# Softmax transpositions as two 64-row halves, and reciprocals broadcast by TensorE instead of by DMA

## The chip, the cores and the metric

The kernel runs on one NeuronCore of one Trainium2 chip. The metric is device time in microseconds for one execution. Besides, one execution was profiled: its span runs from its first to its last instruction.

## The reference

A stack of four graph layers over x of shape (32, 512, 64), in float32, all with one adjacency matrix `adj` (512 x 512). Each layer adds to x a function of h = max(layernorm(x), 0):

- layer 0: `h @ weight_self + adj @ h @ weight_neighbor + bias`
- layer 1: twice `z = relu(adj @ z @ W)`
- layer 2: graph attention. With `Wh = h @ W.T`, the scores are `leaky_relu(e1[i] + e2[j], 0.2)`, masked where adj is not positive; then a softmax over j, the product with Wh, and elu
- layer 3: eight attention heads. Each takes `g = h @ Wh[head]`, scores `(g @ g.T) * adj` with zeros masked, a softmax, and the product with g plus a bias; the heads are joined, go through leaky_relu, and one more layer of the same kind (8 x 128 to 64 features) gives the output, with leaky_relu on top.

So there is one softmax over 512 x 512 scores for each batch entry in layer 2, eight for each in layer 3's heads, and one for each in layer 3's output: 320 in all.

## The kernel before

Layers 0 and 1 run first (the loop from L215), over four groups of eight batch entries. All the rest is a pipeline of 160 *units*: 16 of `Gat` (layer 2, two batch entries each), 128 of `Heads` (two heads of one batch entry) and 16 of `Out` (two batch entries). A unit holds two softmaxes, numbered k = 0 and 1, and takes four steps, one for each block r of 128 score rows.

`run` (L609) writes out the steps of all units, each stage shifted: at a step, one unit makes its scores (`scores`, L469) and, at the end of the step, its row work (`soft`); an earlier one is transposed (`transpose`, L335); a yet earlier one is multiplied with its values (`values`, L348); and an older one is finished (`end`). `prep` readies the unit that comes next. This gives priorities; the framework under the kernel (Tile) then fixes each engine's order, gives out the buffers and sets the semaphores, so that the order in the trace isn't always that of the code.

The work of a flow step (Heads and Out):

- TensorE makes the scores of 128 rows, 2 x 512 columns, into `s_ps`: two matmuls with a contraction of 64, one on each row half of the array (L472). A plain float32 matmul shows as two records in the trace, a transposition as one.
- VectorE multiplies them with adj (`s_att`, L461), makes the mask (L465), and adds both with a row minimum for each k (L325, `finish_rows`).
- ScalarE takes the exponential, with the row sums on the way (L329), into `p_att`.
- For each column block j of 128, `transpose` makes eight 128 x 128 transpositions, four (r) for each k, into a PSUM bank `pt_ps` for each k (L341); ScalarE copies each bank to `pt_att` (L346).
- `values` adds up `av` over j: k = 0 in the first 64 output partitions, k = 1 in the others, so on the two column halves of the array (L353).
- `recips` (L358) is called with the first transposition block (j = 0): the reciprocals of the row sums (`rec`, 128 partitions x 2 x 4, L360) are stored to DRAM (L363) and loaded again, each k as one row of 512, repeated over 64 partitions (`recb`, L366, two loads). Both kinds of DMA are issued on the queue of SyncE (SP), where the stores of the result (L600) stand too.
- `normalize` (L373) multiplies `av` with `recb` to `o_att`. Then Heads makes `y_ps` from it (L544), which ScalarE turns into `cat` (L549).

PSUM has eight banks: two buffers of two banks for `s_ps`, one bank for `av`, and three for everything with the tag "m" (`ps_m`, L266): `pt_ps`, `y_ps`, `g_ps`, `gT_ps` and others.

Of the kernel before, what the change touches and what calls it, by code (L numbers as in the profile page):

```python
# [8 lines left out]
F32 = mybir.dt.float32  # L9
# [5 lines left out]
P = 128  # L15
# [7 lines left out]
def gnn_stack_kernel(  # L23
# [22 lines left out]
    nc = tc.nc  # L46
    B, N, F = x.shape
    C = N // P
# [59 lines left out]
    ident = const.tile([P, P], F32, name="ident")  # L108
# [12 lines left out]
    with tc.tile_pool(name="ps_setup", bufs=2, space=PSUM) as ps:  # L121
        for k in range(C):
            pt = ps.tile([P, N], F32, name="pt")
# [133 lines left out]
    def row_tile(name):  # L257
# [1 line left out]
        return wk.tile([P, N], F32, name=name, tag="row", bufs=2 * H + 6)  # L259

    wk = ctx.enter_context(tc.tile_pool(name="work_b", bufs=2))
    dram = ctx.enter_context(
        tc.tile_pool(name="dram", bufs=3, space=bass.MemoryType.DRAM)
    )
    ps_s = ctx.enter_context(tc.tile_pool(name="ps_s", bufs=2, space=PSUM))
    ps_m = ctx.enter_context(tc.tile_pool(name="ps_m", bufs=3, space=PSUM))  # L266
    ps_v = ctx.enter_context(tc.tile_pool(name="ps_v", bufs=1, space=PSUM))
# [12 lines left out]
    pt = ps_m.tile([P, H, F], F32, name="whT_ps", tag="m")  # L280
# [5 lines left out]
    for h in range(H):  # L286
        nc.tensor.matmul(
            pm[:, h],
            lhsT=whT[:, h].rearrange("p k f -> p (k f)"),
            rhs=whT[:, h, 0],  # L290
            start=True,
            stop=True,
# [12 lines left out]
    def halves(k):  # L305
        return slice(k * F, (k + 1) * F)

    class Pair:
# [26 lines left out]
        def transpose(self, j):  # L335
            pt = pbuf.tile([P, 2, N], F32, name="pt_att", bufs=3)
            self.pts = getattr(self, "pts", []) + [pt]
            for k in range(2):
                ps = ps_m.tile([P, N], F32, name="pt_ps", tag="m")
                for r in range(C):  # L340
                    nc.tensor.transpose(  # L341
                        ps[:, r * P : (r + 1) * P],
                        self.p[:, k, r, j * P : (j + 1) * P],
                        ident,
                    )
                nc.scalar.copy(pt[:, k, :], ps)  # L346

        def values(self, j):  # L348
            pt = self.pts.pop(0)
# [8 lines left out]
        def recips(self):  # L358
            rec = tiny.tile([P, 2, C], F32, name="rec")
            nc.vector.reciprocal(rec, self.sum)  # L360

            row = dram.tile([2, C, P], F32, name="rec_row")
            nc.sync.dma_start(row.rearrange("k r p -> p k r"), rec)  # L363
            self.recb = wk.tile([P, N], F32, name="recb")
            for k in range(2):
                nc.sync.dma_start(  # L366
                    self.recb[halves(k), :],
                    row[k : k + 1].rearrange("k r p -> k (r p)").to_broadcast([F, N]),
                )

        def normalize(self):
            self.o = wk.tile([P, N], F32, name="o_att")
# [236 lines left out]
    def run(units):  # L609
        units = units + [None] * 3  # L610

        def at(k, off):
            u, j = divmod(k - off, C)
            return (units[u], j) if 0 <= u < len(units) else (None, j)

        for j in range(C):
            units[0].prep(j)
        for k in range(len(units) * C):
            cur, r = at(k, 0)
            if cur:  # L620
                cur.scores(r)
            u, j = at(k, C + LAG)
            if u:
                u.transpose(j)
                if j == 0:
                    u.recips()
            u, j = at(k, C + LAG + 1)
            if u:
                u.values(j)
            u, j = at(k, 2 * C + LAG + 1)  # L630
            if u:
                u.end(j)
            u, j = at(k, -C)
            if u:
                u.prep(j)
            if cur:
                cur.soft(r)
# [4 lines left out]
    for b in range(B):  # L642
# [4 lines left out]
        if b % 2 == 1:  # L647
            due.append(((b + 1, 2), b - 1))
    order += [None, None, None, Out(B - 2)]
    run(order)  # L650


# [33 lines left out]
```

## Time and profile before

| What | Value |
|---|---|
| Median of 3 runs | 3047.99 us (3045.97 to 3050.04) |
| The profiled execution's own time | 3050.04 us |
| Its span | 3048.1 us |
| TensorE, busy share of the span | 90% (12972 matmul records) |
| VectorE | 80% (4802 instructions) |
| ScalarE | 63% (4426) |
| Mean granted TensorE clock | 0.955 |
| `pt_ps` transpositions (L341) | 5120, 738.4 us busy |
| `pt_att` copies (L346) | 1280, 578 ns each |
| `rec` (L360) | 160, 201 ns each |
| DMAs `rec_row` and `recb` | 160 and 320, 10.5 and 3.2 us from issue to landing |

The kernel has stages with different limits: layers 0 and 1 until about 460 us, Gat until about 705 us, heads and outputs until about 2985 us, and an end in which the last Out unit has nothing beside it. A line of the page's groups gives the code line, engine, operation, tiles written and read, shapes and count, then busy time and mean duration, then the idle time of the engine just before. In the timeline a row begins with its start and its length in microseconds. "PEld" is TensorE's loading of weights, which goes on beside its matmuls. TensorE's busy time is that of overlapping records whose ends are modelled: the time from one start to the next tells more.

### The profile page before, as it was taken

The numbers are of one execution on the slowest core, as the hardware profiler recorded it, in microseconds if no ns is written. First come the engines' busy times: TensorE is split into PE (matmuls) and PEld (weight loads), VectorE is DVE, ScalarE is ACT, GpSimd is POOL, SyncE is SP. The second block draws the span as 40 slices with busy tenths as digits, with TensorE's granted clock in tenths as the row PEclk, the third lists the DMA queues.
The fourth block names the chain that finished last, engine by engine and source line by source line (L and its number), as shares of the span: only waits on it lengthen the run. The fifth ranks groups of instructions, "written<-read, shape, count | busy, mean of one in ns | idle before, by whom it ended". The sixth has DMA issues, their size and how long they took to land.

```text
span 3048.1 us, 37087 instructions
## 1 busy us (share of the span) xinstructions
PE 2753.6 (90%) x12972; PEld 1251.4 (41%) x12972; DVE 2425.9 (80%) x4802; ACT 1933.2 (63%) x4426; POOL 99.5 (3%) x49
## 2 busy tenths in 40 slices
PE   4674667888899999999999999999999999999996
PEld 2332334444344444444444444444444444444442
DVE  5325337899898988889898989888898989898893
ACT  0110115667687777777777777777777777777773
POOL 3102100000000000000000000000000000000000
PEclk9887887899899999999999999999999999999998
DMA  3000000000110111111110101111011101011010
GB/s 82 0 0 0 0 0 8 15 15 15 15 22 15 25 18 18 22 18 22 18 22 18 22 18 22 20 20 18 19 22 18 22 18 22 18 22 22 18 22 14
DMA packets 201851, 55.42 MB, mean 18 GB/s; under 512 B 172488, under 2 KB 180848, under 8 KB 201536
## 3 DMA queue, kind: packets, MB, share of 16 engines
q1 hardware_dynamic: 198832, 49.97, 10.1%
q8 instruction: 101, 1.65, 0.3%
q10 hardware_dynamic: 2080, 2.10, 0.2%
q14 instruction: 86, 0.70, 0.2%
q0 software_dynamic: 752, 0.99, 0.2%
HBM read 48.17 MB, written 4.85 MB: 17 GB/s over the span
## 4 chain that ended last, share of the span: by engine, by line
DVE 55%; PE 24%; ACT 13%; issue 5%; DMA 2%; POOL 1%; POOLq 0%; DVEq 0%; SPq 0%; ACTq 0%
DVE t_att L325 18%; DVE s_att L461 14%; DVE t_att L465 8%; ACT p_att L329 8%; PE nt_ps L195 6%; PE av L353 3%; PE pt_ps L341 3%; DVE o_att L373 3%; ACT cat L549 3%; PE s_ps L472 3%; PE gT_ps L567 3%; PE po L206 2%; DVE l_att L432 2%; DVE hn L164 1%; DVE l_att L325 1%
## 5 line engine op out<-in xcount | busy, mean ns | idle before, releaser
L329 ACT ACTIVATE p_att<-t_att,negmax 128x512 f32<-128x512 f32 x1152 | 824.0, 716 | 459.7 <-DVE negmax L325 459.0
L461 DVE TENSOR_TENSOR s_att<-s_ps,adj_p 128x1024 f32<-128x1024 f32 x576 | 702.9, 1220 | 118.6 <-PE s_ps L472 118.6
L341 PEld LDWEIGHTS pt_ps<-ident,p_att 128*128 128x128 f32 x5120 | 554.2, 142 | 547.6 <-issue 230.5
L341 PE MATMUL pt_ps<-ident,p_att 128*128 128x128 f32 x5120 | 738.4, 283 | 28.1 <-ACT cat L549 10.5
L325 DVE CUSTOM_DVE_ANT_0 t_att<-s_att,t_att 128x512 f32<-128x512 f32 x1152 | 752.3, 687 | 13.3
L346 ACT COPY pt_att<-pt_ps 128x512 f32<-128x512 f32 x1280 | 678.6, 578 | 120.9 <-PE pt_ps L341 120.6
L472 PE MATMUL s_ps<-hx,g 64*128 64x512 f32 x2048 | 679.7, 627 | 1.4 <-DVE s_att L461 1.4
L353 PE MATMUL av<-pt_att,hn 128*64 128x512 f32 x2048 | 571.3, 618 | 0.7 <-DVE o_att L373 0.7
L465 DVE TENSOR_SCALAR t_att<-s_att 128x1024 f32<-128x1024 f32 x576 | 393.2, 683 | 24.5 <-ACT pt_att L346 0.9
L472 PEld LDWEIGHTS s_ps<-hx,g 64*128 64x128 f32 x2048 | 214.0, 186 | 310.6 <-issue 104.8
L329 ACT ACTIVATION_READ_ACCUMULATOR p_att<-t_att,negmax 128x1 f32 x1152 | 216.0, 188 | 0.0
L195 PE MATMUL nt_ps<-adj_t,hn 128*128 128x512 f32 x256 | 134.9, 668 | 60.5 <-DVE hn L168 60.5
L199 ACT COPY nt<-nt_ps 128x512 f32<-128x512 f32 x48 | 28.1, 585 | 237.6 <-PE nt_ps L195 237.6
L544 PE MATMUL y_ps<-o_att,wh_sb 64*128 64x512 f32 x512 | 163.1, 645 | 6.0 <-DVE o_att L373 4.1
L549 ACT ACTIVATE cat<-y_ps,bh 128x512 f32<-128x512 f32 x256 | 159.4, 671 | 8.8 <-PE y_ps L544 8.8
L353 PEld LDWEIGHTS av<-pt_att,hn 128*64 128x64 f32 x2048 | 105.8, 135 | 97.2 <-issue 89.7
L246 DVE SCALAR_TENSOR_TENSOR x<-po,x 128x256 f32<-128x256 f32 x32 | 12.1, 419 | 167.5 <-PE po L206 167.5
L516 PE MATMUL g_ps<-hx,m 64*128 64x512 f32 x256 | 143.7, 641 | 0.0
L373 DVE TENSOR_TENSOR o_att<-av,recb 128x512 f32<-128x512 f32 x160 | 109.5, 684 | 32.5 <-DMA recb<-rec_row 29.0
L152 ACT ACTIVATE std<-var,eps 128x32 f32<-128x32 f32 x16 | 5.1, 321 | 189.3 <-DVE var L150 189.3
L567 PE MATMUL gT_ps<-cat,wo_sb 128*64 128x512 f32 x512 | 122.6, 602 | 0.0
L360 DVE RECIPROCAL rec<-sum_att 128x8 f32<-128x8 f32 x160 | 32.1, 201 | 111.7 <-ACT p_att L329 111.7
(114 smaller groups left out, 2015.4 us busy)
## 6 DMA issues: line engine op xcount, KB each, us to landing
recb<-rec_row SPq DMA_DIRECT2D x320, 128.0 KB, 3.2
out_dram<-x SPq DMA_DIRECT2D x32, 128.0 KB, 10.1
rec_row<-rec SPq DMA_DIRECT2D x160, 4.0 KB, 10.5
x<-in_x_dram ACTq DMA_DIRECT2D x2, 1024.0 KB, 23.5
x<-in_x_dram SPq DMA_DIRECT2D x2, 1024.0 KB
adj_raw<-in_adj_dram SPq DMA_DIRECT2D x1, 1024.0 KB
wh_sb<-in_L_gnn_Wh_dram POOLq DMA_DIRECT2D x2, 256.0 KB, 7.8
wo_sb<-in_L_gnn_W_out_dram POOLq DMA_DIRECT2D x1, 256.0 KB, 8.3
```

What stands on the lines that cost most here:

```text
L195: nc.tensor.matmul(p, lhsT=lhs(k), rhs=adj_t[:, k, :], start=(k == 0), stop=(k == C - 1))
L325: nc.vector.tensor_tensor_reduce(out=ns[k], in0=s[k], in1=t[k], scale=-1.0, scalar=BIG, op0=OP.add, op1=OP.min, accum_out=self.negmax[:, k ...
L329: nc.scalar.activation(self.p[:, k, r, :], ns[k], AF.Exp, bias=self.negmax[:, k, r : r + 1], scale=-1.0, accum_out=self.sum[:, k, r : r + 1],)
L341: nc.tensor.transpose(ps[:, r * P : (r + 1) * P], self.p[:, k, r, j * P : (j + 1) * P], ident,)
L346: nc.scalar.copy(pt[:, k, :], ps)
L353: nc.tensor.matmul(self.av[halves(k), :], lhsT=self.v(k, j), rhs=pt[:, k, :], start=(j == 0), stop=(j == C - 1),)
L373: nc.vector.tensor_tensor(self.o, self.av, self.recb, OP.mult)
L461: nc.vector.tensor_tensor(s, ps, adj_f[:, r, None, :].to_broadcast([P, 2, N]), OP.mult)
L465: nc.vector.tensor_scalar(t, s, 0.0, FLOW_NEG, op0=OP.is_equal, op1=OP.mult)
L472: nc.tensor.matmul(u.s_ps[:, k], lhsT=g[halves(k), r * P : (r + 1) * P], rhs=x[halves(k), :], start=True, stop=True,)
L549: nc.scalar.activation(cat, ps, AF.Prelu, bias=bh[:, h : h + 1], scale=1.0, alpha=0.01)
L567: nc.tensor.matmul(self.gps[halves(k), :], lhsT=wo_sb[:, h, :], rhs=Heads.cat[b + k, h], start=(h == 0), stop=(h == H - 1),)
```

## The change

Two things change. First, each 128 x 128 transposition becomes two of 64 rows: rows 0 to 63 of `p_att` on the first row half of TensorE, rows 64 to 127 on the second, issued in turn. Each half has its own PSUM bank, which now holds both k, so two of ps_m's banks are written side by side; ScalarE still makes two copies of 512 columns, now one for each half, and each writes runs of 64 elements. Second, the reciprocals no longer go through DRAM. Eight matmuls a unit, with a column of `rec` repeated 64 times as the stationary operand and the identity as the moving one, put them on 64 partitions for each k, in a bank of ps_m, and ScalarE copies that bank to `recb`. `recips` is called with the second block (j = 1) instead of the first, after its transpositions. The DRAM pool goes.

```diff
         def transpose(self, j):
             pt = pbuf.tile([P, 2, N], F32, name="pt_att", bufs=3)
             self.pts = getattr(self, "pts", []) + [pt]
+
+            ps = [ps_m.tile([P, 2, C, F], F32, name="pt_ps", tag="m") for half in range(2)]
             for k in range(2):
-                ps = ps_m.tile([P, N], F32, name="pt_ps", tag="m")
                 for r in range(C):
-                    nc.tensor.transpose(
-                        ps[:, r * P : (r + 1) * P],
-                        self.p[:, k, r, j * P : (j + 1) * P],
-                        ident,
-                    )
-                nc.scalar.copy(pt[:, k, :], ps)
+                    for half in range(2):
+                        nc.tensor.transpose(
+                            ps[half][:, k, r],
+                            self.p[halves(half), k, r, j * P : (j + 1) * P],
+                            ident[halves(half), halves(half)],
+                        )
+            pth = pt.rearrange("p k (r half q) -> p k r half q", r=C, half=2)
+            for half in range(2):
+                nc.scalar.copy(pth[:, :, :, half, :], ps[half])
...
             nc.vector.reciprocal(rec, self.sum)
-
-            row = dram.tile([2, C, P], F32, name="rec_row")
-            nc.sync.dma_start(row.rearrange("k r p -> p k r"), rec)
+            ps = ps_m.tile([P, N], F32, name="rec_ps", tag="m")
+            for r in range(C):
+                for k in range(2):
+                    nc.tensor.matmul(
+                        ps[halves(k), r * P : (r + 1) * P],
+                        lhsT=rec[:, k, r : r + 1].to_broadcast([P, F]),
+                        rhs=ident,
+                        start=True,
+                        stop=True,
+                    )
             self.recb = wk.tile([P, N], F32, name="recb")
-            for k in range(2):
-                nc.sync.dma_start(
-                    self.recb[halves(k), :],
-                    row[k : k + 1].rearrange("k r p -> k (r p)").to_broadcast([F, N]),
-                )
+            nc.scalar.copy(self.recb, ps)
...
                 u.transpose(j)
-                if j == 0:
+                if j == 1:
                     u.recips()
```

More of the change, by code (lines that the diff above doesn't have):

```diff
@@ L261, in gnn_stack_kernel @@
     wk = ctx.enter_context(tc.tile_pool(name="work_b", bufs=2))
-    dram = ctx.enter_context(
-        tc.tile_pool(name="dram", bufs=3, space=bass.MemoryType.DRAM)
-    )
     ps_s = ctx.enter_context(tc.tile_pool(name="ps_s", bufs=2, space=PSUM))
@@ L360, in recips @@
             nc.vector.reciprocal(rec, self.sum)
-            row = dram.tile([2, C, P], F32, name="rec_row")
-            nc.sync.dma_start(row.rearrange("k r p -> p k r"), rec)
-            self.recb = wk.tile([P, N], F32, name="recb")
-            for k in range(2):
-                nc.sync.dma_start(
-                    self.recb[halves(k), :],
-                    row[k : k + 1].rearrange("k r p -> k (r p)").to_broadcast([F, N]),
-                )
+            ps = ps_m.tile([P, N], F32, name="rec_ps", tag="m")
[8 more added lines that the diff above has]
+                    )
+            self.recb = wk.tile([P, N], F32, name="recb")
+            nc.scalar.copy(self.recb, ps)
         def normalize(self):
```

## The prediction

> **What bounds the kernel now.** I read the page's slices first, to find the stages.
>
> ```profile
> PE   4674667888899999999999999999999999999996
> DVE  5325337899898988889898989888898989898893
> ACT  0110115667687777777777777777777777777773
> ```
>
> From slice 10 on nothing changes: that is the softmax over heads and outputs, about 705 to 2985 us. TensorE (PE) stands at 9 throughout, VectorE (DVE) at 8 to 9, ScalarE (ACT) at 7. So I asked for busy times in the middle of that stage, for all work and then for the transpositions alone; the columns are PE, PE's weight loads, DVE, ACT, POOL, then clock and DMA (the second row: PE, weight loads, ACT).
>
> ```profile
> 1000.00:2500.00 1500.00, 1485.12 (x7238) 641.96 (x7236) 1320.08 (x2616) 1132.91 (x2618) 0.00 (x0) 1.00 0.13 20
> 1000.00:2500.00 1500.00, 437.62 (x3096) 329.83 (x3096) 407.66 (x774) 1.00 0.13 20
> ```
>
> 3096 transpositions at eight a step are 387 steps, so a step lasts 1500/387 = 3.876 us. In it PE is busy 3.84, DVE 3.41, ACT 2.93. PE is the bound, with DVE 11% behind. The waits of the same window say what stops DVE:
>
> ```profile
> DVE rec L360 <- ACT p_att L329: 77.5, 87, 2.1
> DVE s_att L461 <- PE s_ps L472: 75.2, 97, 2.1
> PE pt_ps L341 <- ACT cat L549: 7.6, 24, 0.5
> ```
>
> Of DVE's 180 us of idle time, 77.5 (0.20 a step) is the reciprocal waiting for an exponential and 75.2 (0.19) is waiting for scores from PE; the other 27 (0.07) are gaps between dependent operations. PE hardly waits. DVE's own floor is therefore 3.41 + 0.07 = 3.48 us a step.
>
> Then the timeline, a step with nothing extra in it, to see how PE spends its time:
>
> ```profile
> 1537.29 0.20 DVE L360 RECIPROCAL rec<-sum_att 128x8 f32<-128x8 f32 x1 [0.69 <-ACT p_att L329]
> 1537.63 1.13 PE L472 MATMUL s_ps<-hx,g 64*128 64x512 f32 x4
> 1538.69 1.09 PE L341 MATMUL pt_ps<-ident,p_att 128*128 128x128 f32 x8
> 1539.72 1.08 PE L353 MATMUL av<-pt_att,gV 128*64 128x512 f32 x4
> 1540.72 1.13 PE L472 MATMUL s_ps<-hx,g 64*128 64x512 f32 x4
> 1540.72 0.30 PEld L472 LDWEIGHTS s_ps<-hx,g 64*128 64x128 f32 x4 [0.81 <-DVE s_att L461]
> ```
>
> Scores, transpositions and values take 1.06 + 1.03 + 1.00 = 3.09 us back to back, in three array shapes: 64 rows, 128 by 128, 64 columns. In the single records the two halves of a score start 6 to 8 ns apart, their weight loads too: 4 loads of 185 ns fill 0.30 us. A transposition follows the last by 0.109 us. The last score record to the first transposition is 0.520, where a 512-column record needs 0.43 (the spacing of the weight loads of L195): the change of shape costs 0.09. The first transposition then takes 0.166, and the last is followed by the values after 0.202, again 0.09 over.
>
> One place already has the form that the change uses, a 64-row transposition, on one row half:
>
> ```profile
> L282 PEld LDWEIGHTS whT_ps<-ident,wh_sb x8: 136/138/143, 451.1 to 451.5; 64*128 64x128 f32 x8
> L282 PE MATMUL whT_ps<-ident,wh_sb x8: 221/223/244, 451.1 to 451.6; 64*128 64x64 f32 x8
> ```
>
> Each is one matmul record, and their starts are 0.062 us apart.
>
> **What the Trainium skill says.** "TensorEngine Tiling (Array Packing)", section "Key Properties": changing the tiling mode drains TensorE, and different tiles load weights and multiply in parallel. The trace agrees with both: 0.09 us at each change of shape, and score halves that start 6 to 8 ns apart. Its section "Gotcha 1: PSUM Pressure" says that row tiles write to different banks; the scores do so already. "TensorE: Matmul & The Clock Gate", section "Step-by-step: what each phase is for", gives a 64-deep queue from which weight loads are pulled ahead; the 6 to 8 ns after long matmuls fit. Its section "Wait — 56ns, not 53.3ns?" gives about 62 ns per matmul when the sequencer decodes in software. That is the whT pitch too, and those eight came straight after a blocking wait; so no row here tells whether 62 ns is the array or the sequencer.
>
> **The change part by part**, per step.
>
> *Transpositions.* Out: 8 of 0.109 with their switch in. From the last score record to the first value record there are 0.520 + 0.166 + 6 x 0.109 + 0.202 = 1.54 us, less 0.43 for the score itself: 1.11. In: 16 halves in 8 pairs, in the score's own shape, so no drain before them: 7 x 0.062 + (0.062 + 0.09) = 0.59. Saved: 0.53. Unknown is whether two halves overlap in transpose mode. If fully, 0.59; if not at all, 15 x 0.062 + 0.15 = 1.08, and 0.03 is saved. I take the first, because the score halves overlap in loads and matmuls and the shape is the same; the 32 instructions are queued behind a 1.06 us score. The shape changes from transposed to plain matmuls at one array size cost nothing in the trace (0.111 from e_ps to pt_ps).
>
> *ACT's copies* stay two of 0.58, now to runs of 64 elements; no row shows that form, so 0 to 10% more (an estimate), and I take 0: ACT has 0.9 us of slack in a step. The first copy began after four transpositions (0.5 us) and now begins after all sixteen (0.5 us as well).
>
> *Banks.* A step's transpositions need two of ps_m's three banks at their start, where the second was needed half-way. In the step after y_ps this waits for cat already now (7.6 us in 387 steps). All 16 then wait, but they need only 0.5 after it where the four left needed 0.43: about nothing. If ACT is late elsewhere, up to 0.1 a step.
>
> *Reciprocals on PE.* Eight matmuls a unit, two records each by the pattern of the other plain matmuls, 128 columns at 0.109: 16 records, in pairs on the two column halves as L353's values run, 8 x 0.109 = 0.87 us a unit, 0.22 a step (0.44 if the pairs don't overlap). They stand before the values, in their shape: no further switch. ACT gains one copy of 0.58 a unit, 0.15 a step.
>
> *The wait that this adds.* The first of them waits for DVE's reciprocal; behind it in PE's queue stand values, g_ps and the next scores, and for those waits DVE's s_att. The timeline has the reciprocal between s_att and t_att of a step, early; and recips moves from j = 0 to j = 1, a step later. So PE should find it done. The same move may shrink the 0.20 wait of the reciprocal on ACT; I keep 0.14 of it.
>
> *DMAs.* One store and two loads a unit leave SP's queue; SP then holds only the stores of out. They were hidden but for three places:
>
> ```profile
> DVE o_att L373 <- DMA recb<-rec_row: 29.0, 3, 14.2
> 3041.41 0.69 DVE L373 TENSOR_TENSOR o_att<-av,recb 128x512 f32<-128x512 f32 x1 [14.24 <-DMA recb<-rec_row]
> ```
>
> At the last the values were done at 3035.15, so 6.3 us were the DMA's; at 2999.89 3.4 were. With PE's 0.9 in their place: 8 us saved in all.
>
> **The sum.** PE's floor becomes 3.84 - 0.53 + 0.22 = 3.53, DVE's stays 3.48, ACT's is 3.07. Two engines within 0.05 of each other, with steps that differ (y_ps and g_ps add about 1 us to two of four), don't both run full. I put the step at DVE's 3.48 + 0.14 (reciprocal) + 0.07 (a third of the wait for scores) = 3.69: 0.185 less. Between 705 and 2985 us there are 4680/8 = 585 steps: 108 us. The Gat stage (460 to 705 us) has DVE busy 211 of 245 us, and its PE work isn't the bound: 0, within 10. The span is 3048.1 - 108 - 8 = 2932. The profiled execution took 3050.0, 2 us more than its span and 2 more than the median of the runs, so the median to expect is 2932 too.
>
> **Rivals.** (1) *The halves don't overlap*, or the sequencer feeds one in 62 ns. PE: 3.84 - 0.03 + 0.22 + 0.04 = 4.07, 0.19 more, 585 times: +111 - 8, 3151 us. For it: no transposed pair is in the trace, and whT's 62 ns. Against it: the scores. It decides once a pair takes over 0.105 us; there the gain is gone. (2) *The reciprocal's wait takes the place of the DMA*: if DVE has it behind the whole row work of the step before, PE may only do that step's scores and transpositions (1.06 + 0.59) under it. A unit is then 4 x 3.53 - 1.65 + 3.1 (row work) + 0.2 + 0.3 for hand-overs = 16.1 us against 15.5: 0.14 a step, 3130 less 8, about 3120. It decides when PE waits over 1.4 us a unit. Against it: the reciprocal's place at 1537.29. (3) *DVE keeps all its waits or the three banks bind*: step 3.80 to 3.86, 2995 to 3042 us. (4) *Both engines run full*: 3.56, 2855 us; the lower end.
>
> **How the numbers follow.** Likeliest, halves overlap and DVE takes over, 0.67, with its own range of 2855 to 2995; (3) 0.08; no change 0.03 (within 0.2%, 6 us, about what a measurement of this kernel can tell from none); (1) 0.13; (2) 0.09. Faster 0.75, same 0.03, slower 0.22. The range 2860 to 3080 leaves out 0.03 below, (1), and a part of (2).
>
> **What would show it.** Right: 16 records of pt_ps in about 0.55 us with pairs 6 to 8 ns apart, 0.43 from the last score to the first of them, PE busy below 3.7 a step, and DVE with the highest share. Wrong: half records spaced 0.06 singly (1); PE idle at the new matmuls before a reciprocal (2); pt_ps waiting on pt_att, g or cat for over 0.1 a step (3). An order of instructions that differs much from today's would upset the sum in ways that I can't price.

## The result, and the profile after

The changed kernel takes 3201.45 us (median of 4 runs, 3199.80 to 3202.94), the kernel before in the same comparison 3048.57: **1.050 times as long** (95% interval 1.048 to 1.052). I had forecast 2932. The profiled execution took 3201.84 us, its span 3200.1.

The slices of the page show that no engine is full any more; from slice 10 on TensorE stood at 9 before.

```profile
PE   4666578778888889888889888888888898989887
DVE  5334438889878887878887888878788878888884
```

The middle of the long stage, all work and then the transpositions alone (columns as in the prediction):

```profile
1000.00:2500.00 1500.00, 1324.11 (x11086) 649.34 (x11082) 1234.20 (x2439) 1093.84 (x2530) 0.00 (x0) 1.00 0.01 3
1000.00:2500.00 1500.00, 324.05 (x5792) 268.97 (x5790) 381.91 (x722) 1.00 0.01 3
```

5792 halves at 16 a step are 362 steps of 4.144 us, where before there were 387 of 3.876. TensorE is busy 161 us less in the window, and the steps are 0.27 longer all the same. The waits of that window say what filled the time:

```profile
DVE rec L361 <- ACT p_att L326: 169.7, 80, 2.1
PE g_ps L520 <- ACT pt_att L347: 89.4, 80, 1.2
DVE s_att L465 <- PE s_ps L476: 68.9, 91, 2.6
PE pt_ps L340 <- ACT pt_att L347: 43.3, 70, 0.7
PE pt_ps L340 <- ACT cat L553: 37.8, 70, 0.9
```

Two things are new. VectorE stands at the reciprocal 0.47 us a step (169.7/362) where it stood 0.20, about 2.1 us for each of 80 units; its wait for scores is what it was (0.19). And TensorE, which hardly waited, now waits for banks of ps_m: `g_ps` and `pt_ps` until ScalarE has emptied one. The page's group of the reciprocals has the first over the whole span, with the idle time ahead of them at the end of the row:

```profile
L361 DVE RECIPROCAL rec<-sum_att 128x8 f32<-128x8 f32 x160 | 32.2, 201 | 266.8 <-ACT p_att L326 266.8
```

The same row of the kernel before ended in 111.7. The 155 us more are about what the kernel lost, though the runs below show that they are not all of it. The timeline shows one such place; rows that play no part in it are left out:

```profile
1018.13 0.69 DVE L322 CUSTOM_DVE_ANT_0 t_att<-s_att,t_att 128x512 f32<-128x512 f32 x1
...
1018.68 0.59 PE L476 MATMUL s_ps<-hx,g 64*128 64x512 f32 x1
...
1018.97 1.25 ACT L553 ACTIVATE cat<-y_ps,bh 128x512 f32<-128x512 f32 x2
1019.69 0.71 PE L340 MATMUL pt_ps<-ident,p_att 64*128 64x64 f32 x15 [0.42 <-ACT cat L553]
1020.11 0.71 ACT L326 ACTIVATE p_att<-t_att,negmax 128x512 f32<-128x512 f32 x1
...
1020.95 0.20 DVE L361 RECIPROCAL rec<-sum_att 128x8 f32<-128x8 f32 x1 [2.12 <-ACT p_att L326]
1021.07 1.17 DVE L465 TENSOR_TENSOR s_att<-s_ps,adj_p 128x1024 f32<-128x1024 f32 x1
```

VectorE ends a unit's last row block at about 1018.8. The next instruction in its queue is that unit's reciprocal, which needs the row sums of the block's second exponential, and that one stands behind two `cat` activations on ScalarE (1.25 us). The first of these also keeps TensorE's transpositions from their second bank, 0.42 us. The scores of the next block are there by 1019.27 as the record models it, yet `s_att` starts at 1021.07, because it is behind the reciprocal. The Trainium skill, "TensorE: Matmul & The Clock Gate", section "Architectural detail: the array is 16× 32×32, not 1× 128×128", says that VectorE's queue is strict first in, first out; these rows agree. In the kernel before (the prediction's row at 1537.29) `s_att` stood ahead of the reciprocal and covered the wait but for 0.69. In the instruction order of VectorE the reciprocal stood between an `s_att` and its `t_att` in 126 of 160 units before; after, directly ahead of the next unit's `s_att` in 124.

### The profile page after: what moved, and what is told of

Read it like the earlier page. It is cut to its first block, busy times and chain, and to the rows that moved or that the text cites. A ratio compares the mean times of both kernels' runs of the same rounds, so it can differ in the third digit from the quotient of the medians.

```text
span 3200.1 us, 51783 instructions
## 1 busy us (share of the span) xinstructions
PE 2642.8 (83%) x20652; PEld 1339.2 (42%) x20652; DVE 2432.6 (76%) x4802; ACT 2002.8 (63%) x4586; POOL 99.0 (3%) x49
## 4 chain that ended last, share of the span: by engine, by line
DVE 48%; PE 27%; ACT 20%; issue 4%; POOL 1%; DMA 0%; POOLq 0%; DVEq 0%; ACTq 0%
DVE s_att L465 15%; DVE t_att L322 12%; ACT p_att L326 12%; DVE t_att L469 9%; PE nt_ps L195 6%; PE s_ps L476 4%; ACT cat L553 4%; PE g_ps L520 3%; PE av L354 3%; PE gT_ps L571 3%; DVE o_att L377 2%; ACT pt_att L347 2%; PE po L206 2%; PE pt_ps L340 2%; DVE hn L164 1%
## 5 line engine op out<-in xcount | busy, mean ns | idle before, releaser
L340 PE MATMUL pt_ps<-ident,p_att 64*128 64x64 f32 x10240 | 588.2, 228 | 165.8 <-ACT pt_att L347 74.5
L340 PEld LDWEIGHTS pt_ps<-ident,p_att 64*128 64x128 f32 x10240 | 486.9, 139 | 551.0 <-issue 181.1
L476 PE MATMUL s_ps<-hx,g 64*128 64x512 f32 x2048 | 704.6, 625 | 6.5 <-DVE s_att L465 6.5
L354 PE MATMUL av<-pt_att,hn 128*64 128x512 f32 x2048 | 578.9, 613 | 0.8 <-DVE o_att L377 0.7
L476 PEld LDWEIGHTS s_ps<-hx,g 64*128 64x128 f32 x2048 | 240.8, 186 | 286.4 <-issue 73.2
L365 PE MATMUL rec_ps<-ident,rec 128*64 128x128 f32 x2560 | 180.9, 284 | 17.1 <-ACT p_att L326 11.7
L548 PE MATMUL y_ps<-o_att,wh_sb 64*128 64x512 f32 x512 | 193.9, 643 | 0.9 <-DVE o_att L377 0.9
L365 PEld LDWEIGHTS rec_ps<-ident,rec 128*64 128x64 f32 x2560 | 142.0, 139 | 37.8 <-ACT pt_att L347 14.9
L520 PEld LDWEIGHTS g_ps<-hx,m 64*128 64x128 f32 x256 | 37.7, 184 | 253.0 <-ACT pt_att L347 250.7
L571 PE MATMUL gT_ps<-cat,wo_sb 128*64 128x512 f32 x512 | 132.9, 595 | 0.0
```

What stands on the lines that cost most here:

```text
L340: nc.tensor.transpose(ps[half][:, k, r], self.p[halves(half), k, r, j * P : (j + 1) * P], ident[halves(half), halves(half)],)
L354: nc.tensor.matmul(self.av[halves(k), :], lhsT=self.v(k, j), rhs=pt[:, k, :], start=(j == 0), stop=(j == C - 1),)
L365: nc.tensor.matmul(ps[halves(k), r * P : (r + 1) * P], lhsT=rec[:, k, r : r + 1].to_broadcast([P, F]), rhs=ident, start=True, stop=True,)
L476: nc.tensor.matmul(u.s_ps[:, k], lhsT=g[halves(k), r * P : (r + 1) * P], rhs=x[halves(k), :], start=True, stop=True,)
L520: nc.tensor.matmul(ps, lhsT=m2[rows, 2 * i : 2 * i + 2, :].rearrange("p h f -> p (h f)"), rhs=self.x[rows, :], start=True, stop=True,)
```

## The experiments

The first batches set **Theory P**, that the place of the reciprocal in VectorE's order makes the loss, against **Theory B**, that three banks in ps_m do. Later runs set P against **Theory M**, that the place only moves a wait. Each batch of experiments was timed together with the kernel before on one chip (3038 to 3040 us there), and gains and losses below are against that; the first two rows of the table are from the comparison above. The step and the two waits are those of the window 1000 to 2500 us, in us a step.

| Run | Transpositions | Reciprocals | Their place on VectorE | Median us | Ratio to before (95%) | Step | Wait at rec | Wait for scores |
|---|---|---|---|---|---|---|---|---|
| before | whole | DMA | behind next s_att | 3048 | 1 | 3.876 | 0.20 | 0.19 |
| after | halves | TensorE | ahead of next s_att | 3201 | 1.050 (1.048 to 1.052) | 4.144 | 0.47 | 0.19 |
| e1 | halves | TensorE | two row blocks later | 3159 | 1.040 (1.038 to 1.042) | 4.084 | 0 | 0.49 |
| e2 | halves | DMA | ahead of next s_att | 3141 | 1.034 (1.032 to 1.035) | 4.054 | 0.48 | 0.10 |
| e3 | whole | TensorE | behind next s_att | 3112 | 1.025 (1.023 to 1.026) | 3.990 | 0.12 | 0.38 |
| e4 | whole | DMA | one row block later | 3024 | 0.995 (0.994 to 0.997) | 3.846 | 0 | 0.31 |
| e5 | halves | DMA | one row block later | 2989 | 0.983 (0.981 to 0.984) | 3.778 | 0 | 0.25 |
| e6 | halves | TensorE, two steps later | two row blocks later | 3099 | 1.020 (1.018 to 1.021) | 3.968 | 0 | 0.39 |
| e7 | whole, both banks at once | DMA | behind next s_att | 3043 | 1.001 (1.000 to 1.002) | 3.886 | 0.16 | 0.24 |
| e8 | whole | DMA | ahead of next s_att | 3166 | 1.042 (1.041 to 1.044) | 4.098 | 0.50 | 0.12 |
| e9 | halves | TensorE | behind next s_att | 3079 | 1.014 (1.012 to 1.015) | 3.947 | 0.10 | 0.35 |
| e10 | halves | DMA | behind next s_att | 3022 | 0.995 (0.993 to 0.996) | 3.834 | 0.14 | 0.23 |
| e11 | halves | DMA, and the matmuls | one row block later | 3095 | 1.019 (1.017 to 1.021) | 3.947 | 0 | 0.39 |
| e12 | halves, y_ps apart | DMA | one row block later | 2934 | 0.965 (0.964 to 0.967) | 3.676 | 0 | 0.19 |
| e13 | whole, y_ps apart | DMA | behind next s_att | 3079 | 1.013 (1.012 to 1.015) | 3.942 | 0.06 | 0.34 |
| e14 | halves, y_ps apart | TensorE | behind next s_att | 3019 | 0.994 (0.992 to 0.995) | 3.838 | 0.11 | 0.24 |

### Each half of the change alone, and the reciprocal held back

`e1_pin` holds the reciprocal of the changed kernel where the code calls it:

```diff
-            nc.vector.reciprocal(rec, self.sum)
+            tc.keep_in_program_order(nc.vector.reciprocal(rec, self.sum))
```

> The changed kernel with one edit: the reciprocal is held behind everything written before it on VectorE, two row blocks after its unit's last one, where now it stands directly behind that last one. Theory P (the place of the reciprocal in VectorE's order makes the loss): its wait for the exponential (0.47 us a step) goes, scores may be waited for a little more; step 3.65 to 3.85, time 2920 to 3030. Theory B (the three PSUM banks make it: PE waits 0.47 us a step for copies): the wait only moves from the reciprocal to s_att; time 3140 to 3210.

`e2_half` has the half transpositions of the change with the DMAs of the kernel before; `e3_rec` the whole transpositions of the kernel before with the change's matmuls, copy and `j == 1`.

> The half transpositions alone, reciprocals by DMA as before. The reciprocal stands before the next s_att in 123 of 160 units, as in the changed kernel. Theory P: it waits there about 2.1 us a unit, so most of the loss is here too; 3080 to 3190. Theory B: without a fourth user of the three banks PE's saving shows; 2900 to 3000.

> The reciprocals by TensorE alone, whole transpositions as before. The reciprocal stands behind s_att in 126 of 160 units, as in the kernel before. Theory P: PE, which was full, gets 0.22 us a step more: 3048 + 585 x 0.22 - 8 = 3170, with no new wait at the reciprocal. Theory B: 0.2 to 0.4 us of bank waits a step on top; 3250 to 3400.

e1 gained 1% only: it misses Theory P's range and lies in Theory B's. VectorE no longer waits at the reciprocal (its wait for scores rose from 0.19 to 0.49 a step instead), but TensorE does. Two rows of the waits, then the timeline of one unit:

```profile
PE rec_ps L365 <- ACT p_att L326: 109.9, 82, 1.9
PE pt_ps L340 <- ACT pt_att L347: 3.8, 11, 0.4
```

```profile
1547.42 0.20 DVE L361 RECIPROCAL rec<-sum_att 128x8 f32<-128x8 f32 x1
1547.76 1.09 PE L365 MATMUL rec_ps<-ident,rec 128*64 128x128 f32 x16 [1.83 <-ACT p_att L326]
```

The wait names an exponential, but the matmuls start 0.14 us after the end of the reciprocal, behind a whole row block, and the exponential of that unit had long been done: it is the reciprocal that TensorE waits for. That is the prediction's rival (2), made by the experiment; the changed kernel itself doesn't have it. Theory B's cause isn't what holds e1 up: TensorE's waits for `pt_att` copies, 89.4 and 43.3 us in the changed kernel, are down to 3.8, though that for `cat` grew from 37.8 to 58.6.

e2 is where P had it, with the wait of the changed kernel (0.48 a step) and without a matmul of the new kind: the half transpositions alone bring the reciprocal ahead of `s_att`. e3 doesn't have that wait, and loses 74 us on a TensorE that is full (busy 1498 of 1500 us): less than P's sum, and far less than B's. So each half of the change costs time by itself, and for different reasons.

### The reciprocal held back without the broadcasts

`e4_before_pin` and `e5_half_pin` put e1's edit on the kernel before and on e2. `e6_split` keeps the matmuls and ScalarE's copy of the change but issues them at j = 3, with the reciprocal still held at j = 1. `e7_before_two_banks` only takes both banks of the whole transpositions at once, and copies both after all eight (the start of the edit is shown):

```diff
-            for k in range(2):
-                ps = ps_m.tile([P, N], F32, name="pt_ps", tag="m")
-                for r in range(C):
+            ps = [ps_m.tile([P, N], F32, name="pt_ps", tag="m") for k in range(2)]
+            for r in range(C):
+                for k in range(2):
```

> The kernel before with the reciprocal held in the order of the code, one row block later. Both theories: PE is the bound there, so the reciprocal's 0.20 us a step goes but little is gained: 3020 to 3050. If it gains over 40 us, VectorE's wait at the reciprocal was already a bound of the kernel before.

> The half transpositions alone, reciprocals by DMA, and the reciprocal held in the order of the code, one row block later, so that nothing on VectorE waits for an exponential and nothing on TensorE for the reciprocal. Theory P (the loss of the changed kernel is its reciprocal: on VectorE where it stands early, on TensorE where it stands late): PE's floor is 3.31 us a step, VectorE's 3.48; step 3.55 to 3.75, 2870 to 2975. Theory B (holding two of the three banks at once is the loss): PE waits 0.3 us a step and more for copies and VectorE for scores; 3060 to 3150.

> The changed kernel with the reciprocal held in the order of the code and its eight matmuls and their copy written two steps later (with the fourth block of transpositions), so that TensorE finds the reciprocal done. Theory P: no wait at either place; step 3.6 to 3.8, 2900 to 3000. Theory B: as with the reciprocal held alone, 3120 to 3170.

> The kernel before, with whole transpositions, but both banks of a step taken at its start and written in turn, and both copied after all eight; the reciprocal stands where it stood before, behind s_att, in 125 of 160 units. Theory P: the hold of the banks costs little, as TensorE is full anyway; 3040 to 3080. Theory B: TensorE waits for copies 0.2 to 0.4 us a step; 3150 to 3280.

e4 and e7 are where P had them. e5 beats the kernel before by 1.7%: half transpositions pay once the reciprocal is out of the way, 35 us against e4, though less than P's range had it. e6, which waits for the reciprocal nowhere, is 110 us above e5. It too is above P's range, and both are below B's: the place of the reciprocal isn't all of it. e7 costs nothing: two banks at once are not a loss by themselves with whole transpositions, and they don't move the reciprocal either.

### The place alone

`e8_before_early` is the kernel before with one order changed: the reciprocal is called as soon as its unit's last row block is written, and the next `s_att` is queued behind it. The second part of the edit:

```diff
-        nc.vector.tensor_tensor(
-            s, ps, adj_f[:, r, None, :].to_broadcast([P, 2, N]), OP.mult
-        )
+        with tc.issue_after(last[0].ins) if last else contextlib.nullcontext():
+            nc.vector.tensor_tensor(
+                s, ps, adj_f[:, r, None, :].to_broadcast([P, 2, N]), OP.mult
+            )
```

`e9_after_late` does the reverse to the changed kernel, and `e10_half_late` to e2: the reciprocal is called between `s_att` and `t_att` of the next unit's first step (`early` is the reciprocal, held in that order; a part of the edit).

```diff
+        for w in waiting:
+            w.early()
+        del waiting[:]
         t = wk.tile([P, 2, N], F32, name="t_att", bufs=3)
```

`e11_half_matmuls` adds to e5 the eight matmuls of the change at j = 3, with nothing that reads them.

> The kernel before, with one edit: on VectorE's queue the reciprocal stands directly behind its unit's last row block and ahead of the next s_att, where the changed kernel has it (139 units of 160); transpositions and DMAs stay. Theory P (place of the reciprocal): its wait for the exponential grows from 0.20 to 0.45 or more a step as in the changed kernel, and most of it reaches the end: 3110 to 3200 us. Theory M (the place only moves a wait: what VectorE loses at the reciprocal it gets back at the wait for scores, because TensorE is the bound here): wait for the exponential 0.45 a step, wait for scores near 0, 3040 to 3080 us.

> The changed kernel, with one edit: the reciprocal is fixed between the next unit's first s_att and its t_att, where the kernel before has it; broadcast by TensorE at j = 1 stays. Theory P: VectorE's wait for the exponential falls from 0.47 to 0.1 to 0.2 a step and TensorE does not wait for the reciprocal (unlike with the reciprocal behind a whole row block); what stays of the loss is the 110 us that the broadcasts cost in the split kernel, less what half transpositions gain: 3060 to 3120 us. Theory M: the waits move elsewhere and the time stays at 3150 to 3200 us.

> Half transpositions alone, reciprocals by DMA, the reciprocal fixed between the next unit's first s_att and its t_att. Theory P: 2985 to 3040 us, since the reciprocal waits 0.7 us a unit at most, against none in the kernel where it stands behind a whole row block (2989) and 2.1 where the framework places it (3141). Theory M: 3080 us or more.

> Half transpositions, reciprocals by DMA behind a row block (2989 us), and besides the eight broadcast matmuls of each unit at j = 3, into a bank of ps_m that nothing reads (no copy on ScalarE; the result of these matmuls is not used). If TensorE's time is what the broadcasts cost (0.22 a step, 110 us in the split kernel): 3070 to 3105 us. If it is ScalarE's copy and the bank that waits for it: 2990 to 3020 us.

e8, e9 and e10 came out as P had it, and e11 as forecast if TensorE's time is what the broadcasts cost. Rows of the waits, e8 first, then e9:

```profile
DVE rec L363 <- ACT p_att L332: 183.6, 92, 2.1
DVE s_att L468 <- PE s_ps L480: 44.3, 30, 2.1
```

```profile
DVE s_att L473 <- PE s_ps L487: 133.6, 180, 4.4
PE g_ps L531 <- ACT pt_att L349: 74.6, 85, 1.2
DVE rec L363 <- ACT p_att L328: 39.7, 75, 0.6
```

In e8 the new place costs the kernel before 128 us, with not one matmul added. VectorE gets back little of it at the scores (0.19 to 0.12 a step), so Theory M falls, although TensorE is 99% busy in the kernel before. How the stall reaches TensorE the traces show only in part. The two `y_ps` matmuls of a unit, which run side by side on the two row halves in the kernel before, are mostly torn apart in e8, the second waiting for a bank that a `pt_att` copy holds: in 95 of 128 units, against 17 before. One such place of e8, and TensorE's, its weight loads' and ScalarE's busy time with `y_ps` in the window, first in the kernel before, then in e8:

```profile
1505.82 1.12 PE L552 MATMUL y_ps<-o_att,wh_sb 64*128 64x512 f32 x2
1507.13 0.69 PE L552 MATMUL y_ps<-o_att,wh_sb 64*128 64x512 f32 x1 [0.18 <-ACT pt_att L349]
```

```profile
1000.00:2500.00 1500.00, 109.52 (x348) 32.68 (x348) 108.31 (x174) 1.00 0.13 20
1000.00:2500.00 1500.00, 151.08 (x327) 42.23 (x326) 102.01 (x164) 1.00 0.10 19
```

With four records a unit that is 1.26 us a unit before and 1.85 in e8. What share of the 128 us goes this way isn't shown. e10 against e2 doesn't have this difference (2.11 and 2.12 us a unit): there the place alone is worth 119 us, 3.9%. In e9 the mended place brings the changed kernel from 1.050 to 1.014 of the kernel before: 3.7%, some 112 us. An edit of one order can move other instructions too: about 15 of ScalarE's 4426 stand elsewhere in e10 than in e2, and some 200 in e9 than in the changed kernel, so e10 against e2 is the cleaner pair.

e11 is 107 us above e5, as e6 was (110). So at j = 3 it is TensorE's time that the broadcasts cost, not ScalarE's copy.

### The banks

`e12_half_pin_y` is e5 with the two `y_ps` matmuls of a unit issued one step apart, so that one bank fewer is held for a `cat` when the transpositions ask for two:

```diff
-            elif step == 1:
-                for k in range(2):
+            elif step in (1, 2):
+                for k in [step - 1]:
```

`e13_before_y` and `e14_after_y` put the same edit on the kernel before and on the changed kernel.

> Half transpositions, reciprocals by DMA behind a row block (2989 us), and one edit: the two y_ps matmuls of a unit are issued one step apart, so that only one of the three banks is held for a cat when the next transpositions ask for two. If that bank is what keeps half transpositions from their forecast gain: the wait of pt_ps for cat falls from 58 us in 1500 to under 15 and the time by 35 to 60 us, to 2930 to 2955 us. If the limit is the pace between scores on TensorE and row work on VectorE, which each wait for the other in steps of unequal length: the wait falls too, but the time by less than 15 us, 2975 to 2995 us.

> The kernel before, with the one edit that a unit's two y_ps matmuls are issued one step apart. If the edit helps because half transpositions ask for two banks at once: whole ones ask for the second bank only half-way and wait 7.6 us in 1500 for cat, so at most 12 us to gain, 3025 to 3045 us. If it helps whatever the transposition (steps of more equal length): 2980 to 3005 us.

> The changed kernel, with the one edit that a unit's two y_ps matmuls are issued one step apart. In the order that results, the framework puts the reciprocal behind the next s_att in 126 units of 160, as in the kernel before. If the place of the reciprocal, the banks and the broadcasts' time on TensorE are all of the loss: 2934 us, plus 10 to 30 for a reciprocal that waits 0.7 us a unit, plus 57 to 110 for the broadcasts: 3000 to 3070 us, with VectorE's wait at the reciprocal under 0.25 a step and pt_ps waiting for cat under 15 us in 1500. If something else is in it: above 3080 us.

e12 is the best kernel of the study, 2934 us, 55 less than e5. In e5's waits and timeline the cause was

```profile
PE pt_ps L343 <- ACT cat L553: 57.9, 76, 0.9
```

```profile
1535.24 1.12 PE L548 MATMUL y_ps<-o_att,wh_sb 64*128 64x512 f32 x2
1536.73 0.69 PE L548 MATMUL y_ps<-o_att,wh_sb 64*128 64x512 f32 x1 [0.38 <-ACT pt_att L350]
...
1539.62 0.71 PE L343 MATMUL pt_ps<-ident,p_att 64*128 64x64 f32 x15 [0.91 <-ACT cat L553]
```

The second `y_ps` waits for a bank that a `pt_att` copy holds, then fifteen of the next step's sixteen transpositions wait for `cat`. In e12's longest waits pt_ps no longer waits for cat; the `y_ps` has what is left of it (25.0 us).

e13 went against both expectations: the edit makes the kernel before 41 us slower. Its timeline shows a reason; first the step of the kernel before that has the `y_ps`, then one of e13:

```profile
1533.34 1.14 PE L544 MATMUL y_ps<-o_att,wh_sb 64*128 64x512 f32 x4
1534.30 1.03 PE L472 MATMUL s_ps<-hx,g 64*128 64x512 f32 x4
1535.27 1.43 PE L341 MATMUL pt_ps<-ident,p_att 128*128 128x128 f32 x8
```

```profile
1540.21 0.69 PE L544 MATMUL y_ps<-o_att,wh_sb 64*128 64x512 f32 x1
1540.22 0.69 PE L472 MATMUL s_ps<-hx,g 64*128 64x512 f32 x1
...
1542.12 1.09 PE L341 MATMUL pt_ps<-ident,p_att 128*128 128x128 f32 x8
```

From the first `y_ps` to the transpositions it is 1.93 us with a pair of `y_ps`, which lies on both row halves, and 1.91 with a single one: a single one takes as long as a pair, and e13 has two of them a unit. A full TensorE pays for that, but the rows give the direction and not the size: beside a score's own 1.06 us, two singles in place of one pair are 0.83 us more, 106 us in 128 units, an estimate from these rows, where 41 were lost. VectorE's wait at the reciprocal also fell, from 0.20 to 0.06 a step. In e5 the pair was already torn apart by the wait for a bank (the rows at 1535.24 and 1536.73), so e12 had nothing to lose.

e14 is the change whole, with one edit, 0.6% faster than the kernel before (0.994, against 1.050 for the change as it was). With this edit the framework puts the reciprocal behind `s_att` again, in 126 units, so e14 mends both the place and the bank; e9, which mends only the place, lies 61 us above it.

## Why the prediction was wrong

By its own steps, point by point. First a part of a step of the changed kernel, for the first two points, then TensorE's busy time with `y_ps` in e9 and in e10, for the second:

```profile
1541.62 0.66 PE L340 MATMUL pt_ps<-ident,p_att 64*128 64x64 f32 x16
1542.21 1.07 PE L354 MATMUL av<-pt_att,hn 128*64 128x512 f32 x2
1543.01 1.15 PE L365 MATMUL rec_ps<-ident,rec 128*64 128x128 f32 x16
1543.93 0.59 PE L354 MATMUL av<-pt_att,hn 128*64 128x512 f32 x1
```

```profile
1000.00:2500.00 1500.00, 128.55 (x340) 49.23 (x340) 105.88 (x170) 1.00 0.01 3
1000.00:2500.00 1500.00, 183.69 (x348) 50.93 (x348) 108.37 (x174) 1.00 0.12 20
```

- **Transpositions: right.** Sixteen halves take 0.59 us to the values (1541.62 to 1542.21), as forecast. In the single records the two of a pair start 6 to 12 ns apart, pairs follow each other by 0.062, and the last score record is 0.422 ahead of the first. Rival (1) is refuted. ScalarE's copies to runs of 64 elements take 580 ns, 578 before: the 0 taken for them was right too.
- **Reciprocals on PE: the duration was right, the price low.** From the first of the sixteen records to the values it is 0.92 us, for 0.87 forecast. But I let 0.22 a step vanish under VectorE as the next bound. It cost 58 us where the place is as before (e9 less e10) and 107 to 110 at j = 3 (e11 and e6 less e5), out of 129 (585 times 0.22) if it had been paid in full. Why the two positions differ no run tests. One reason is in the traces: e10's `y_ps` pairs are mostly torn (2.11 us a unit) and e9's mostly not (1.51), so that the order of e9 gives TensorE 0.60 us a unit back, while e5, e6 and e11 have them torn alike (2.11 to 2.14). On the full TensorE of the whole transpositions it cost 74 (e3).
- **The wait that this adds: here the prediction failed.** I took the reciprocal's place from one row of the timeline and kept it, and even let its wait shrink from 0.20 to 0.14 by the move to j = 1. The move did nothing: with j = 1 and whole transpositions (e3) the reciprocal stands behind `s_att` as before, with j = 0 and halves (e2) ahead of it. So it is the half transpositions that put it on the other side. It waited 0.47. By e9 this is 3.7% of the 5.0% lost; the same flip is 3.9% between e10 and e2, and 4.2% on the kernel before (e8). What in the framework's choice flips it isn't known; taking two banks at once isn't enough (e7).
- **Banks: the sign was right, the size not.** "About nothing, up to 0.1 a step" was 0.22 at `pt_ps` alone (43.3 and 37.8 us in 362 steps), and 0.25 more at `g_ps`, which I hadn't listed: `rec_ps` takes the third bank just ahead of it. Removing the cat part is worth 55 us (e12) and, with the broadcasts, 61 (e14 against e9). The Trainium skill's "Gotcha 1: PSUM Pressure" of "TensorEngine Tiling (Array Packing)", which I had cited, says that row tiling increases PSUM pressure. The traces agree: here each half holds a bank until ScalarE's copy.
- **DMAs: right in size.** VectorE's wait for `recb` at three places (29.0 us) became one for `av` at three (23.1): 6 us saved, 8 forecast.
- **The sum.** A saving on the bound engine was booked as time until the next engine's floor. e5 and e10 show what halves give with the old waits in place: 16 to 35 us, not 108. The largest part of what is missing that a run has shown is the wait for a bank: freeing it (e12) gives 55 more, where two engines that pace each other in steps of unequal length were expected to allow under 15. Only then does the step reach 3.68; that this is near the 3.69 I gave is chance, since e12 has no broadcasts. A slip of the arithmetic besides: rival (3)'s upper end of 3.86 a step comes to 3031 us by the same sum, not 3042.

The account of the loss, in per cent of the kernel before: halves in the old order −0.5 (e10), broadcasts +1.9 (e9 against e10), place of the reciprocal +3.7 (after against e9): +5.0. The shares depend on the order in which the parts are put together: with the reciprocal in its new place the broadcasts are +1.7 (after against e2). Of the forecast's cases none came about. Rival (3)'s signature was there, but it was bounded by today's order; the case that happened was the sentence at the end of the prediction, that another order of instructions would upset the sum, and that had been given no chance.

## What to carry to other kernels

Where a framework orders the instructions, any edit can move others that it doesn't touch: before costing an edit, look for the instructions whose wait is covered only by what happens to stand ahead of them, price the wait without that cover (here 2.1 us a unit against 0.9), and fix their place. Compare the other engines too after such a fix: e8 moved one reciprocal and tore TensorE's pairs apart. A transposition split on row halves needs its banks at the same moment, so its gain is decided by who holds the other banks. And on engines that hand buffers to each other, time taken from the bound engine is worth what the waits between them let through, a third of the sum here until the bank was freed.

## What the runs showed of the hardware

- Two 64-row transpositions of float32, 64 columns each, run side by side on the two row halves: a pair every 0.062 us, so an instruction every 31 ns. The 62 ns per matmul that the prediction held possible as a limit of the sequencer were none here. The first half of a step starts 0.422 us after the last score record, where a whole transposition, in another array shape, starts 0.520 after it.
- A single matmul on one row half between paired scores takes the room of a pair: 1.91 us against 1.93 in the rows of e13 and of the kernel before.
